# The first output projection's loads in another order, half of y kept in SBUF, and one norm's root moved to VectorE

## The chip, the cores and the metric

The kernel runs on one core of one Trainium2 chip. The metric is the device time of one execution in microseconds, and of several runs the median. Before the change the runs gave 3252.81, 3256.49 and 3258.94 us, so the median is 3256.49 us. Engines are named as the profile names them: PE is TensorE, DVE is VectorE, ACT is ScalarE, POOL is GpSimd, SP is SyncE, which here does nothing but issue transfers.

## The reference

`x` is (4, 1024, 512) in float32. One decoder block is computed: a Mamba layer with its MLP, a cross-attention on a context of 64 tokens, and a feed-forward layer with low-rank experts. A layer norm of the sum with the input closes each of the three. The change touches the first of them, which in short is:

```python
def _mamba(x, ...):
    xz = x @ in_proj_w.T
    u, z = jnp.split(xz, 2, axis=-1)               # 1024 features each
    u_act = silu(causal_conv(u))
    dt_r, Bm, Cm = jnp.split(u_act @ x_proj_w.T, [32, 48], axis=-1)
    dt = softplus(dt_r @ dt_proj_w.T + dt_proj_b)
    dA = exp(dt * A)                               # 16 states
    dBu = dt * Bm * u_act
    h_t = dA_t * h_{t-1} + dBu_t                   # lax.scan over the tokens
    y = sum_n(hs_n * Cm_n) + u_act * Dp
    return (y * silu(z)) @ out_proj_w.T
h = x + _mamba(_rmsnorm(x, norm1_w), ...)
xn = _rmsnorm(h, norm2_w)
h = h + (silu(xn @ w1.T) * (xn @ w2.T)) @ w3.T
```

`_rmsnorm` multiplies by the reciprocal root of the mean square plus 1e-5, and by a weight.

## The kernel before

**Chunks, groups, steps, quarters.** The 4096 tokens are worked on as 8 chunks `c` of 512. The 1024 features are two halves of 4 blocks of 128. One chunk and one half make a group `g = 2c + half`; one group and one of the 16 states make a step `k = 16g + n`, so there are 256 steps. A step has 4 quarters, one per block of features (and per block of 128 tokens). Quarters are counted through in `now[0]`, and this count is called a slot: slot = 4k + quarter.

**One quarter** is the function `quarter(k, q, other)`, and it does, in this order: PE turns a block of the step before (`turn`, tile `ps_h`), `other()` gives PE work of the MLP, DVE does one scan of 512 tokens (`scan`, tile `hs`, with the decay `da` as input), ACT makes a decay two blocks ahead (`exp`, tile `da`) and in some quarters puts in the state carried over (`carry_in`), the turned block is multiplied by C and added up in `acc`, and in the first two quarters POOL makes the input product of the next step (`times_b`, 128x1024 elements). Of the additions into `acc` most are made by DVE from PSUM; for some, ACT first makes the tile `hc` and POOL adds it, or PE adds it when turning back (tables `JS0`, `AS0`, `JS`, `AS`).

**The order is written out by hand.** `InOrder` ties each instruction of PE, ACT, DVE and POOL to the one issued before it on the same engine, so these four run in program order, and every instruction has the line number of that helper (308) in the profile. Transfers issued by SP are not tied; the scheduler places them, and SP's queue then runs in its order. Work for a later slot is registered with `at(d, phase, f)` and is run in the named phase of the quarter `d` slots later; the table `NP` has these delays for the MLP.

**The end of a group.** `end()` turns the sums back to features by tokens (`ps_y`), `add_u` on DVE adds the skip term, giving the tile `y`, and `times_z` on POOL multiplies by the gate. Then a transfer issued by ACT's queue one slot later writes the 128x512 tile to DRAM (`dr["y"]`, 256 KB); there are 64 of these in the run.

**The MLP stream.** `stream()` is a generator; each element is a group of matmuls with a cost, and `paced` hands out at most two per quarter while their cost stays under a budget (`PACE`). It makes for each chunk an `Mlp`, whose `__init__` loads `h` (1 MB, the chunk's `x`, line 854), whose `load_o` loads four tiles `wo` of 512 KB of the out projection's weight (line 869), and whose `load_y` reads back the chunk's `y` in four tiles `wy` of 512 KB (line 874). `wy` shares a ring of 5 buffers with the tiles `w12` of the MLP's weights (line 972). `out_proj` multiplies (`ps_o`, 4 blocks of tokens by 8 of features), then come the residual (`norm_h`, DVE, tile `hn`), the squares (`norm_sq`, ACT), the reciprocal root (`norm_r`, POOL, by `rsqrt_p`: a first guess from the bits and three Newton steps, on 128x4 elements), the scaling (`norm_x`, ACT), the addition (`norm_add`, POOL, tile `h`) and the turns (`turns`, tile `xn`). The first `Mlp` is made at slot 161:

```python
def stream():
    yield from until(GJ * 2 * NS + 33)
    mlp = Mlp(0)
```

The `Mlp` of a later chunk is made inside `run` of the one before, and its out projection starts at slot 128(c+1) + 21 or after. The last chunk's MLP runs after the scan, interleaved with the attention.

**Memory around the first MLP.** Up to step 39 the first chunk's turned-back parts `hc` are held in a pool of 44 buffers (`hz`), with a PSUM pool of its own (`zp`). It is closed after that step, and the pools of the MLP (`wp`, `xp`, `gp`, `sm`, `pp`) are opened in its place; a load into a tile there waits until the former user of the space has been read.

**Other lines that matter.** `load_b` (line 704) loads `b`, a row spread over 128 partitions; `load_uz` (line 787) loads skip and gate; `rsqrt_v` (line 189) is the root on DVE, with 12 small operations, and `rsqrt_p` (line 206) that on POOL, with 13.

Of the kernel before, what the change touches and what calls it, by code (L numbers as in the profile page):

```python
# [10 lines left out]
F32 = mybir.dt.float32  # L11
# [3 lines left out]
ALU = mybir.AluOpType  # L15
# [4 lines left out]
P = 128  # L20
B, L, D = 4, 1024, 512
N = B * L
KD = D // P
DI, KI = 1024, 8
NS = 16
DTR = 32
T = 512
NT = T // P
NC = N // T
# [108 lines left out]
for g, first in enumerate((4, 6)):  # L138
    for n in range(1, 16):
        for t in range(4):  # L140
            i = 4 * (n - 1) + t
# [8 lines left out]
EARLY_STEPS = 4  # L150
# [9 lines left out]
def f32(t):  # L160
    return t.bitcast(F32)
# [15 lines left out]
def rsqrt(nc, pool, out, v, tag):  # L177

    shape = list(out.shape)
    r = pool.tile(shape, F32, tag=tag + "r", name="rs_r")  # L180
    w = pool.tile(shape, F32, tag=tag + "w", name="rs_w")
    nc.scalar.activation(r, v, AF.Ln)
    nc.scalar.activation(r, r, AF.Exp, scale=-0.5)
    nc.vector.tensor_tensor(w, v, r, ALU.mult)
    nc.vector.tensor_tensor(w, w, r, ALU.mult)
    nc.vector.tensor_scalar(w, w, -0.5, 1.5, ALU.mult, ALU.add)
    nc.vector.tensor_tensor(out, r, w, ALU.mult)
# [18 lines left out]
def rsqrt_p(nc, pool, out, v, tag):  # L206

    shape = list(out.shape)
    r = pool.tile(shape, F32, tag=tag + "r", name="rs_r")
    w = pool.tile(shape, F32, tag=tag + "w", name="rs_w")  # L210
    nc.gpsimd.tensor_scalar(
        r.bitcast(I32), v.bitcast(I32), -0.5, float(0x5F3759DF), ALU.mult, ALU.add
    )
    for i in range(3):
        nc.gpsimd.tensor_tensor(w, r, r, ALU.mult)
        nc.gpsimd.tensor_tensor(w, w, v, ALU.mult)
        nc.gpsimd.tensor_scalar(w, w, -0.5, 1.5, ALU.mult, ALU.add)
        nc.gpsimd.tensor_tensor(out if i == 2 else r, r, w, ALU.mult)
# [43 lines left out]
def tokens(d, c, t=T):  # L262

    return d[c * t : (c + 1) * t].rearrange("(t p) d -> p t d", p=P)
# [17 lines left out]
def open_pool(tc, name, bufs, **kw):  # L282
    return tc.tile_pool(name=name, bufs=bufs, reuse_waits="tile", **kw)
# [374 lines left out]
def scan_mlp(tc, cn, a, dr, before, bx, then):  # L658
# [5 lines left out]
    nc = pin  # L664
    ident = cn["ident"]
    GJ = 4
    with ExitStack() as ctx, ExitStack() as sx:
# [8 lines left out]

        carry = cp.tile([P, KI, NS], F32, tag="carry", name="carry")
        pks, bs, cts, accs, hcs, uzs, firsts = {}, {}, {}, {}, {}, {}, {}
        zps, tw = [], []

        class Step:


            def __init__(self, k):
                self.k = k
                self.g, self.n = divmod(k, NS)
                self.c, self.half = divmod(self.g, 2)
                self.first = self.c % (L // T) == 0
                self.by_add, self.by_turn = (AS0[self.g], JS0[self.g]) if self.g < 2 else (AS, JS)
                self.da = {}  # L690
# [141 lines left out]

            def times_z(self, i, y):
                nc.gpsimd.tensor_tensor(y[1], y[1], uzs.pop((self.g, i))[:, 1], ALU.mult)
                jp, jj = divmod(GJ * self.half + i, 2)
                at(1, 3, nc.scalar.dma_start, dr["y"][self.c][jp][:, jj], y[1])
                if i < 2:
                    at(1, 3, self.load_uz, i + 2, nc.scalar)

        def at(d, phase, f, *args):  # L840

            due.setdefault((now[0] + d, phase), []).append(lambda: f(*args))
# [5 lines left out]
        class Mlp:  # L848


            def __init__(self, c):
                self.c = c
                self.h = xp.tile([P, NT, D], F32, tag="h", name="h", bufs=2)
                nc.sync.dma_start(self.h, tokens(a["x"], c))
                self.ws, self.ps, self.gs, self.w3s = {}, {}, {}, []

            def w3_tile(self, name, late):

                if late:
                    return tw[0].tile([P, 2, D], F32R, tag="w3", name=name)  # L860
                return wp.tile([P, 2, D], F32R, tag="w3", name=name, bufs=4)

            def load_o(self):
                self.wo, self.ys = [], []
                for jp in range(KI // 2):
                    if jp == KI // 4 and self.c == NC - 1:
                        self.load_y()
                    self.wo.append(f32(self.w3_tile("wo", self.c == NC - 1 and jp < 2)))
                    nc.sync.dma_start(self.wo[jp], a["w_out"][:, 2 * jp : 2 * jp + 2])

            def load_y(self):
                for jp in range(KI // 2):
                    self.ys.append(f32(wp.tile([P, 2, T], F32R, tag="w12", name="wy")))
                    nc.sync.dma_start(self.ys[jp], dr["y"][self.c][jp])

# [7 lines left out]
            def out_proj(self):  # L883

                self.ss = sm.tile([P, NT], F32, tag="ss", name="ss")
                self.r = sm.tile([P, NT], F32, tag="nr", name="nr")
                hn = [gp.tile([P, 2, T], F32R, tag="gs", name="hn", bufs=6) for i in range(2)]
                self.hn = [f32(hn[t // 2][:, t % 2]) for t in range(NT)]
                if not self.ys:
                    self.load_y()  # L890
                ys, ws = self.ys, self.wo
                for t in range(NT):
                    ps = pp.tile([P, D], F32, tag="mm", name="ps_o")
                    for j in range(KI):
                        jp, jj = divmod(j, 2)
                        nc.tensor.matmul(
                            ps, ys[jp][:, jj, t * P : (t + 1) * P], ws[jp][:, jj],
                            start=j == 0, stop=j == KI - 1,
                        )
                        if j == KI - 1:  # L900
                            at(*NP["h"], self.norm_h, t, ps)
                            at(*NP["s"], self.norm_sq, t)
                            at(*NP["a"], self.norm_add, t)
                            if t == NT - 1:
                                at(*NP["r"], self.norm_r)
                                for e in range(NT):
                                    at(*NP["x"][e], self.norm_x, e)
                                self.ready = now[0] + NP["t"]
                        yield MM32
# [8 lines left out]
                nc.scalar.activation(sq, self.hn[t], AF.Square, accum_out=self.ss[:, t : t + 1])  # L918

            def norm_r(self):  # L920
                nc.gpsimd.tensor_scalar(
                    self.ss, self.ss, 1.0 / D, 1e-5, ALU.mult, ALU.add
                )
                rsqrt_p(nc, sm, self.r, self.ss, "n")

            def norm_x(self, t):
                nc.scalar.activation(
# [160 lines left out]
        n = NC * 2 * NS  # L1088
# [65 lines left out]
        with ExitStack() as zx:  # L1154
            zps.append(zx.enter_context(open_pool(tc, "b_z", bufs=44, side="right")))
            zps.append(
                zx.enter_context(open_pool(tc, "b_zp", bufs=2, space=PSUM, side="right"))
            )
            for k in range(EARLY_STEPS, 2 * NS + 8):
                for q in range(GJ):  # L1160
                    quarter(k, q, lambda: None)
            turned[0] = 0
        wp = ctx.enter_context(open_pool(tc, "b_w", bufs=5, side="right"))
        xp = ctx.enter_context(open_pool(tc, "b_x", bufs=1, side="right"))
        gp = ctx.enter_context(open_pool(tc, "b_g", bufs=2, side="right"))
        sm = ctx.enter_context(open_pool(tc, "b_sm", bufs=2, side="right"))
        pp = ctx.enter_context(open_pool(tc, "b_p", bufs=3, space=PSUM, side="right"))

        def until(slot):
            while now[0] < slot:  # L1170
                yield 0

        def paced(gen):

            had = [0.0]

            def go():
                had[0] += PACE - TURN * turned[0]
                turned[0] = 0
                for _ in range(2):  # L1180
                    if had[0] <= 0:
                        break
                    cost = next(gen, 0)
                    if not cost:
                        had[0] = 0.0
                    else:
                        had[0] -= cost

            return go

        def first(mlp):
            mlp.load_o()
            yield from mlp.out_proj()
            yield from mlp.turns()

        def stream():
            yield from until(GJ * 2 * NS + 33)
            mlp = Mlp(0)
            yield from first(mlp)
            for c in range(NC - 1):  # L1200
                mlp = yield from mlp.run((lambda: Mlp(c + 1)) if c < NC - 2 else None)

        def last():
            mlp = Mlp(NC - 1)
            yield from first(mlp)
            yield from mlp.run()

        gen = stream()
        m = paced(gen)
        for k in range(2 * NS + 8, n + 2):  # L1210
            for q in range(GJ):
                quarter(k, q, m)

# [17 lines left out]
        sx.close()  # L1231
        tw.append(ctx.enter_context(open_pool(tc, "b_tw", bufs=2, side="right")))
        weave(alone(last()), then(pin, pp))


# [830 lines left out]
```

## Time and profile before

| | |
|---|---|
| median of three runs | 3256.49 us (3252.81 to 3258.94) |
| profiled execution, time | 3250.26 us |
| profiled execution, span | 3248.5 us |
| mean granted clock of PE | 0.959 |
| PE busy | 3001.8 us (92%) |
| DVE busy | 2698.2 us (83%) |
| POOL busy | 2369.2 us (73%) |
| ACT busy | 1973.4 us (61%) |
| transfers | 562.79 MB, mean 173 GB/s |

The profile is of one execution. Its page gives the busy time of each engine, the span in 40 slices of 81 us with the busy share of each engine in tenths, the chain of work that ended last, the costliest groups of instructions, and the transfers' issues. Register, branch and semaphore instructions and the issuing of transfers do not count as busy. Three phases can be told apart in the slices: the in-projection and convolution up to about 490 us, the scan with the MLP beside it up to about 2390 us, and then the last chunk's MLP with the attention and the expert layer. Beside the page, the trace answers for a stretch of time: the timeline of instructions, the waits and what ended them, and the busy time by window.

### The profile page before, as it was taken

What the parts mean: (1) busy time and instruction counts of PE and PEld (TensorE: products, weight loads), DVE (VectorE), ACT (ScalarE), POOL (GpSimd) and SP (SyncE); (2) the same over time, 40 slices, a digit from 0 to 9 for tenths busy, and PEclk for the clock granted to TensorE, in tenths of its full rate; (3) what the DMA queues carried; (4) which work ended last, traced back from release to release, by engine and by line L of the source; (5) the groups of instructions that cost most, each with busy time, mean ns of one, the idle gap of its engine ahead of it and who ended that gap; (6) DMA issues with size and microseconds to landing.
All of it is one profiled execution on the core that took longest, in us unless ns stands there. A gap on an engine that the chain in (4) does not pass through costs nothing.

```text
span 3248.5 us, 47327 instructions
## 1 busy us (share of the span) xinstructions
PE 3001.8 (92%) x15992; PEld 2393.6 (74%) x15992; DVE 2698.2 (83%) x3836; ACT 1973.4 (61%) x3876; POOL 2369.2 (73%) x2169
## 2 busy tenths in 40 slices
PE   7999996887999999999999999999999997999987
PEld 5777773664876786786776786786785887898876
DVE  6876767997999999999999999999962346888876
ACT  3666666776666567666667666667642336666643
POOL 1334328998998999999999999999952115666664
PEclk9999995778999999999999999999999999999998
DMA  4778744336675775675765765765766432111110
GB/s 165 261 264 288 256 167 163 111 104 215 198 224 179 221 223 179 220 226 178 221 223 175 225 217 177 225 213 172 219 190 228 142 104 95 46 46 47 48 41 33
DMA packets 478472, 562.79 MB, mean 173 GB/s; under 512 B 46006, under 2 KB 309814, under 8 KB 477974
## 3 DMA queue, kind: packets, MB, share of 16 engines
q1 hardware_dynamic: 464406, 526.21, 50.6%
q10 hardware_dynamic: 13824, 33.56, 3.2%
q8 instruction: 127, 2.08, 0.3%
q14 instruction: 115, 0.94, 0.1%
HBM read 430.18 MB, written 129.50 MB: 172 GB/s over the span
## 4 chain that ended last, share of the span: by engine, by line
PE 34%; DVE 23%; POOL 12%; issue 8%; DMA 4%; ACT 3%; SPq 0%; ACTq 0%; DVEq 0%; POOLq 0%
DVE hs L308 10%; PE ps_ab L308 10%; POOL hs L308 6%; DVE acc L308 5%; PE ps_m L308 5%; PE ps_h L308 5%; PE ps_o L308 3%; PE ps_s L308 3%; PE ps_b L308 2%; POOL acc L308 2%; PE ps_y L308 2%; DVE g L308 1%; ACT da L308 1%; DMA uz<-pk 1%; DMA w<-w 1%
## 5 line engine op out<-in xcount | busy, mean ns | idle before, releaser
L308 DVE TENSOR_TENSOR_SCAN hs<-da,hs 128x512 f32<-128x512 f32 x1024 | 1214.7, 1207 | 42.7 <-ACT da L308 21.3
L308 POOL TENSOR_TENSOR hs<-pk,b 128x1024 f32<-128x1024 f32 x512 | 1217.2, 2393 | 29.7 <-issue 10.5
L308 ACT ACTIVATE da<-pk,aneg 128x512 f32<-128x512 f32 x1024 | 704.9, 689 | 554.3 <-DVE hs L308 548.6
L308 PE MATMUL ps_ab<-xn,w 128*128 128x512 f32 x3072 | 827.6, 406 | 0.0
L308 PE MATMUL ps_h<-ident,hs 128*128 128x128 f32 x4096 | 684.8, 292 | 91.0 <-DVE hs L308 47.3
L308 PEld LDWEIGHTS ps_h<-ident,hs 128*128 128x128 f32 x4096 | 535.5, 149 | 313.9 <-DVE hs L308 80.5
L308 PEld LDWEIGHTS ps_ab<-xn,w 128*128 128x128 f32 x3072 | 545.0, 189 | 95.8 <-issue 1.1
L308 PE MATMUL ps_m<-w,gs 128*128 128x512 f32 x1536 | 419.3, 408 | 9.5 <-POOL gs L308 9.5
L308 DVE SCALAR_TENSOR_TENSOR acc<-ps_h,c,acc 128x512 f32<-128x512 f32 x542 | 394.2, 727 | 37.8 <-PE ps_h L308 35.6
L308 POOL TENSOR_TENSOR acc<-acc,hc 128x512 f32<-128x512 f32 x232 | 300.1, 1293 | 52.9 <-ACT hc L308 51.5
L308 PEld LDWEIGHTS ps_m<-w,gs 128*128 128x128 f32 x1536 | 274.4, 191 | 61.7 <-POOL gs L308 14.5
L308 PE MATMUL ps_o<-wo,wy 128*128 128x512 f32 x512 | 247.8, 602 | 8.4 <-DMA wy<-y 5.1
L308 ACT ACTIVATE hc<-ps_h,c 128x512 f32<-128x512 f32 x344 | 231.3, 673 | 12.6 <-PE ps_h L308 12.5
L308 POOL TENSOR_TENSOR gs<-g,gs 128x512 fp32r<-128x512 f32 x128 | 165.8, 1295 | 85.1 <-ACT gs L308 85.1
L308 PE MATMUL ps_in<-xn,wu 128*128 128x512 f32 x768 | 214.7, 428 | 0.1
L308 POOL TENSOR_TENSOR pt<-pw,pt 128x512 fp32r<-128x512 f32 x48 | 62.7, 1306 | 194.9 <-ACT pt L308 131.2
L308 PE MATMUL ps_in<-xn,wz 128*128 128x512 f32 x768 | 191.8, 397 | 1.0 <-POOL wz L308 0.6
L308 PEld LDWEIGHTS ps_in<-xn,wu 128*128 128x128 f32 x768 | 145.3, 190 | 56.9 <-issue 22.0
L308 PEld LDWEIGHTS ps_in<-xn,wz 128*128 128x128 f32 x768 | 142.4, 188 | 34.8 <-POOL wz L308 1.1
L308 DVE SCALAR_TENSOR_TENSOR cv<-ps_in,pvec,cv 128x509 f32<-128x509 f32 (+2 forms) x192 | 143.3, 746 | 7.0 <-ACT cv L308 2.3
L308 ACT ACTIVATE hs<-hs,first 128x1 f32<-128x1 f32 x512 | 120.4, 284 | 27.1 <-POOL hs L308 11.7
L308 PEld LDWEIGHTS ps_o<-wo,wy 128*128 128x128 f32 x512 | 87.9, 194 | 66.5 <-issue 65.9
(244 smaller groups left out, 4623.9 us busy)
## 6 DMA issues: line engine op xcount, KB each, us to landing
w<-w SPq DMA_DIRECT2D x384, 512.0 KB, 5.6
b<-b SPq DMA_DIRECT2D x256, 256.0 KB, 4.1
pk<-pk SPq DMA_DIRECT2D x64, 512.0 KB, 6.7
w<-pt SPq DMA_DIRECT2D x48, 512.0 KB, 3.2
pk<-z SPq DMA_DIRECT2D x64, 256.0 KB, 2.9
pk<-u SPq DMA_DIRECT2D x32, 512.0 KB, 3.9
pk<-r SPq DMA_DIRECT2D x32, 512.0 KB, 3.1
pk<-q SPq DMA_DIRECT2D x32, 512.0 KB, 3.7
```

The lines of the kernel that those rows point to most:

```text
L308: ins = f(*args, **kw)
```

## The change

The change has three parts.

1. The first `Mlp`'s loads. It is made at slot 156 instead of 161, and the order of its loads is now `wo`, `wy`, `h` instead of `h`, `wo`, `wy`. Its out projection starts at slot 160 instead of 161. For this, the pools `hz` and `zp` are closed one step earlier.
2. For chunks 0 to 6, the four tiles `y` of the second half of the features are not written to DRAM but kept in SBUF until the out projection reads them there. `load_y` reads back only the first half, in two tiles instead of four. The last chunk goes through DRAM as before.
3. The reciprocal root of the first chunk's MLP norm is made by DVE with `rsqrt_v`, 13 small operations with the one ahead of it, in place of 14 on POOL. The other chunks keep POOL.

```diff
-        zps, tw = [], []
+        zps, tw, kept = [], [], []
...
             def times_z(self, i, y):
                 nc.gpsimd.tensor_tensor(y[1], y[1], uzs.pop((self.g, i))[:, 1], ALU.mult)
-                jp, jj = divmod(GJ * self.half + i, 2)
-                at(1, 3, nc.scalar.dma_start, dr["y"][self.c][jp][:, jj], y[1])
+                if self.half and self.c < NC - 1:
+                    kept.append(y[1])
+                else:
+                    jp, jj = divmod(GJ * self.half + i, 2)
+                    at(1, 3, nc.scalar.dma_start, dr["y"][self.c][jp][:, jj], y[1])
...
             def __init__(self, c):
                 self.c = c
-                self.h = xp.tile([P, NT, D], F32, tag="h", name="h", bufs=2)
-                nc.sync.dma_start(self.h, tokens(a["x"], c))
+                if c:
+                    self.load_h()
...
+            def load_h(self):
+                self.h = xp.tile([P, NT, D], F32, tag="h", name="h", bufs=2)
+                nc.sync.dma_start(self.h, tokens(a["x"], self.c))
...
             def load_y(self):
-                for jp in range(KI // 2):
+
+                for jp in range(KI // 2 if self.c == NC - 1 else KI // 4):
...
-                ys, ws = self.ys, self.wo
+                ws = self.wo
+                ys = [y[:, jj] for y in self.ys for jj in range(2)]
+                while len(ys) < KI:
+                    ys.append(kept.pop(0))
...
-                            ps, ys[jp][:, jj, t * P : (t + 1) * P], ws[jp][:, jj],
+                            ps, ys[j][:, t * P : (t + 1) * P], ws[jp][:, jj],
...
             def norm_r(self):
-                nc.gpsimd.tensor_scalar(
-                    self.ss, self.ss, 1.0 / D, 1e-5, ALU.mult, ALU.add
-                )
-                rsqrt_p(nc, sm, self.r, self.ss, "n")
+                eng, rsqrt = (nc.gpsimd, rsqrt_p) if self.c else (nc.vector, rsqrt_v)
+                eng.tensor_scalar(self.ss, self.ss, 1.0 / D, 1e-5, ALU.mult, ALU.add)
+                rsqrt(nc, sm, self.r, self.ss, "n")
...
-            for k in range(EARLY_STEPS, 2 * NS + 8):
+            for k in range(EARLY_STEPS, 2 * NS + 7):
...
         def first(mlp):
-            mlp.load_o()
             yield from mlp.out_proj()
             yield from mlp.turns()
 
         def stream():
-            yield from until(GJ * 2 * NS + 33)
+            yield from until(GJ * 2 * NS + 28)
             mlp = Mlp(0)
+            mlp.load_o()
+            mlp.load_y()
+            mlp.load_h()
+            yield from until(GJ * 2 * NS + 32)
             yield from first(mlp)
...
         def last():
             mlp = Mlp(NC - 1)
+            mlp.load_o()
             yield from first(mlp)
             yield from mlp.run()
...
-        for k in range(2 * NS + 8, n + 2):
+        for k in range(2 * NS + 7, n + 2):
```

## The prediction

> **What bounds the kernel now.** I read the page from the slices down: where the span is full, and with what. POOL and DVE stand at 9 from slice 12 to slice 30, which is the scan of the state space (about 500 to 2390 us).
>
> ```profile
> span 3248.5 us, 47327 instructions
> ...
> DVE  6876767997999999999999999999962346888876
> ...
> POOL 1334328998998999999999999999952115666664
> ```
>
> Then busy time by stretch. The columns are start:end, length, busy time and instructions of PE, PEld, DVE, ACT and POOL, the granted clock, the DMA share and GB/s.
>
> ```profile
> 740.00:800.00 60.00, 49.33 (x186) 28.23 (x187) 44.23 (x49) 35.20 (x78) 49.11 (x41) 0.81 0.57 183
> 800.00:980.00 180.00, 176.86 (x990) 143.89 (x989) 174.89 (x202) 119.69 (x243) 171.79 (x95) 1.00 0.66 208
> 980.00:1225.00 245.00, 235.75 (x1271) 184.68 (x1270) 234.80 (x274) 155.17 (x297) 232.50 (x157) 0.99 0.67 207
> 1225.00:1469.00 244.00, 236.02 (x1267) 184.85 (x1266) 234.67 (x273) 164.11 (x339) 232.64 (x158) 0.99 0.67 207
> ```
>
> A settled chunk takes 244 to 245 us, with DVE busy for 234.8 and POOL for 232.5: both engines bound it together, PE close behind. One stretch is loose, 740 to 800: DVE 44.23 of 60. There the first output projection and the first MLP norm begin. Next, the waits of 735 to 800 (total, times, longest).
>
> ```profile
> DVE acc L308 <- PE ps_h L308: 9.5, 6, 7.7
> POOL acc L308 <- ACT hc L308: 6.5, 2, 3.8
> DVE hs L308 <- ACT da L308: 5.9, 3, 4.6
> PE ps_o L308 <- DMA wy<-y: 5.1, 2, 4.7
> ```
>
> The reader is to see two stalls: one where PE waits for `wy` (4.7 us) and DVE behind it (7.7), one where DVE waits for ScalarE's `da` (4.6), which turns out to lie behind the norm. In the settled chunks I find neither DVE nor POOL waiting for `wy` or for a write of `y`. So the change can act in these two places, and hardly elsewhere.
>
> **Part 1, the loads' order (first stall).** The timeline (start, duration, engine, operation, idle time before it):
>
> ```profile
> 726.67 0.43 SPq L854 DMA_DIRECT2D h<-in_x_dram  x1
> 727.15 1.59 SPq L869 DMA_DIRECT2D wo<-in_w_out_dram  x2
> 728.85 0.49 SPq L704 DMA_DIRECT2D b<-b  x1
> 729.39 1.22 SPq L869 DMA_DIRECT2D wo<-in_w_out_dram  x2
> 731.15 2.90 SPq L874 DMA_DIRECT2D wy<-y  x3
> ...
> 741.41 3.75 PE L308 MATMUL ps_o<-wo,wy 128*128 128x512 f32 x4 [4.69 <-DMA wy<-y]
> ...
> 748.86 0.75 DVE L308 SCALAR_TENSOR_TENSOR acc<-ps_h,c,acc 128x512 f32<-128x512 f32 x1 [7.72 <-PE ps_h L308]
> ```
>
> SP already sent all of it in one burst from 726.7, since the space of `wo`, `wy` and `h` is that of the in-projection's tiles, which PE's last `ps_y` passes release at 725.9 to 727.0. Those passes stay where they are. So asking five quarters sooner (a quarter here is about 1.75 us: 0.72 for `acc`, 1.21 for a scan less overlap) does not send them sooner; I give this no gain. What changes is the order: `h` (1 MB) goes from first to last, and the third and fourth `wy` are gone. By microsecond from 727 the profile moved 106, 238, 383, 322, 403, 414, 342, 352, 408, 399, 369, 418, 422, 420 and 408 KB, which is 5.2 MB by 741.4. Ahead of the end of the first `wy` now stand four `wo` and itself (2.6 MB), and the `uz`, `b` and `y` that share the 16 engines, put at 0.9 MB: 3.5 MB, which that curve reaches at 737.3; the second `wy` follows at about 738.6. PE gets to the first pass at about 735.6, so it waits until 737.2, not 741.41. From the first pass to the DVE product that had waited took 748.86 - 741.41 = 7.45 us at half clock. One quarter's four `ps_h` (0.60) come on top, the passes standing a quarter earlier in the order: 737.2 + 7.45 + 0.6 = 745.3. That is 3.5 us gained, and the last wait of 0.38 for the fourth `wy` also goes. The ends: 1 us if `uz` and `b` come ahead as much as now, 8.1 if the stall goes wholly (7.72 + 0.38). I take 3.9, by the curve. `h` at the end costs nothing: it is first read at the residual, some 50 quarters later. Two `b` tiles, sent at 728.85 and 736.54, now stand behind `wy`; POOL's products that follow start at 740.62 and 748.89, and no wait of POOL for a transfer is in the list. Bounds 0 to +1, taken 0.
>
> The granted clock was 1.00 until 733, 0.50 from 734 to 747 and 0.97 then: it came back 5.6 us after the passes began at 741.4. I use this row, which moves with the passes. The Trainium skill (TensorE: Matmul & The Clock Gate, Part 1) says the array returns to full rate after about 3.4 us of sustained work; going by it the last 2.2 us at half rate would count for half, and the stall would gain 1.1 us more. The trace's 5.6 us does not agree, and nothing in the sum uses the page.
>
> **Part 2, y in SBUF.** Seven chunks lose 28 issues of `y` on ScalarE's queue (0.33 us each there) and 14 of `wy` on SP (512 KB each), 14 MB in all. Beside: ScalarE is busy for 155 to 164 of 245 us, the DMA engines for 0.67 of the time, and SP is off the path. All DVE waits for ScalarE's `da` come to 21.3 us in the whole run, 6.2 of them in 735 to 800 with the neighbouring ones; 28 x 0.33 = 9.2 us of ScalarE time could take some of the rest, at most 3 us. On the other side, the kept tile of the last block is written by POOL at 735.61 to 736.90, and PE reads it after four passes at the earliest (737.2 + 3.75); if POOL were late, one product of 1.29 us. Bounds -3 to +1.3; taken 0, as no wait in a settled chunk names it. The buffer of `y` is used again 64 quarters later, which leaves no wait.
>
> **Part 3, the norm's root (second stall).** Before, POOL made it in 14 small operations 0.28 us apart, 787.44 to 791.29, and DVE ran on beside it:
>
> ```profile
> 787.44 0.19 POOL L308 TENSOR_SCALAR ss<-ss 128x4 f32<-128x4 f32 x1 [2.79 <-ACT sq L308]
> ...
> 791.33 1.33 ACT L308 ACTIVATE hn<-hn,nr 128x512 f32<-128x512 f32 x2 [1.23 <-POOL nr L308]
> ...
> 796.00 1.22 DVE L308 TENSOR_TENSOR_SCAN hs<-da,hs 128x512 f32<-128x512 f32 x1 [4.62 <-ACT da L308]
> ```
>
> Now 13 small DVE operations stand in DVE's order ahead of the scans that ran from 784.20, and every scan behind them waits for ScalarE's `sq` and for the chain. A free small DVE operation is 0.16 to 0.17 us, 0.20 apart. But elsewhere in this trace such an operation does not run while POOL is in a two-input product:
>
> ```profile
> 3188.14 2.67 POOL L308 TENSOR_TENSOR et<-ef,et 128x512 fp32r<-128x512 f32 x2
> ...
> 3188.54 0.91 DVE L308 TENSOR_SCALAR ln_v<-mv 128x2 f32<-128x2 f32 x1
> ...
> 3189.49 0.17 DVE L308 TENSOR_SCALAR rs_w<-ln_v 128x2 int32<-128x2 int32 x1
> ...
> 3189.69 1.14 DVE L308 TENSOR_SCALAR rs_r<-rs_w 128x2 int32<-128x2 int32 x1
> ```
>
> Each ends when POOL's product ends; one slips in between two products. A 128x1024 product at 144.49 (2.41) held a DVE product from 145.25 for 2.20 us likewise, where others take 0.69. The scans are not held: 1024 of them have a mean of 1207 ns. POOL, rid of the root, goes on with `h` (1.27) and 128x1024 products of 2.35 each: on the clock of before, one ends at 784.65, `h` at 785.9, then 788.25 and 790.6. `sq` ended at 787.35 and now stands a quarter sooner in the order, some 2.3 us here: about 785.0. So: the first operation ends at 786.0, the second slips in, the third ends at 788.3, the fourth slips in, the fifth ends at 790.6, where POOL must wait for a `hc` that needs DVE; eight more at 0.20 give 792.2. The scan of 784.20 then starts at 792.2, 8.0 us late. Idle time that stood there before (0.76 + 4.62 + 0.48 + 0.37 = 6.2) takes part of that back; not all, as ScalarE's `da`, `hc` (0.68 each), `hs` (0.48) and four `hn` (0.67) still come in their order. Followed forward, the scan of 796.00 comes at 801.3 and that of 804.85 at 809.1: 4.3 us lost. The lower end: nothing held, the chain ends at 785.0 + 13 x 0.20 = 787.6 and ScalarE's order sets the rest, -0.6 to +0.4. The upper: one product more in the way, +2.35, so +6.6. I take 4.3, from the rows of the held operations.
>
> The Trainium skill (Perfetto Trace Analysis) warns that moving work between GPSIMD and DVE might not help, as they share a read port. Taken as "no gain" it would put this part at 0, and the sum at -3.9; the rows make it a loss.
>
> **The sum.** -3.9 + 0 + 4.3 = +0.4 us. The profiled execution has a span of 3248.5 and a time of 3250.26; the median of the three runs, 3256.49, is 6.2 (0.19%) above it. 3250.7 as a profiled execution is 3256.9 as a median.
>
> **Rivals.** *Faster: the first stall goes, and the port does not bite.* Place: 735.6. If the first `wy` is there when PE comes, the gain is 8.1. The curve has moved 2.8 MB by 735.6, and four `wo` with one `wy` are 2.6 MB: it needs the queue to let them pass almost alone. Against: `uz` and a `y` leave at 726.30, ahead of them. With the root at its free price (+0.4 to -0.6) and up to 3 from part 2: -7.7 to -11.7, so 3244.8 to 3248.8. For: POOL also waits here (6.5 us for `hc`), and while it waits nothing is held.
>
> *Slower: POOL's products hold the root all the way.* One mechanism: if each product lets only two small operations through, 13 of them need six products, 6 x 2.35 = 14.1 us, not the 7.2 counted; that is 6.9 more, 3263.8. It decides from three further products on (7.05). For: two per product is what the rows show. Against: POOL's `acc` must wait for `hc`, `hc` for `ps_h`, that for a scan, and the scan stands behind the root on DVE; so POOL runs dry after the second or third product.
>
> *The loads do not do what the change says.* If `wo` and `wy` still come behind `h` and `b` through the release of space, part 1 is 0 and the sum +4.3: 3260.8, still within 0.2%.
>
> **How the numbers follow.** 0.2% of the time, 6.5 us, is about what a measurement of this kernel can tell from no change. The likeliest case, both stalls nearly balanced, with the third rival in it: 0.46, 3252 to 3262. The faster rival, or parts of it such as the first stall gone and half of the root's cost: 0.32. The slower: 0.22. The range leaves out a tenth on each side: low, 3245, is the faster rival with all of part 2; high, 3265, is the slower one with the late `b`.
>
> **What would show it.** Right: `wo` before `h` on SP from about 726.7; the first `ps_o` pass near 737; DVE's 7.7 us wait down to about 4; near 785 small DVE operations of 0.9 to 2.3 us that end with POOL products, and scans late by 8; settled chunks of 244 to 245 us as before. Wrong if the small operations all take 0.2 us, if the loads leave before 725, or if a settled chunk is shorter.

## The result and the profile after

The changed kernel takes 3259.75 us (median of 22 runs, 3255.57 to 3267.58), the kernel before 3252.52 us (22 runs beside it, 3249.16 to 3259.30). The ratio is 1.0021, with a 95% interval of 1.0015 to 1.0026: 7.2 us slower by the medians. The prediction's time, 3256.9, and its sum of +0.4 us belong to a time before of 3256.49, the median of the three runs then known. Ratios here and below are the record's; they differ a little from the quotient of the two medians beside them.

The timeline around the first stall, after the change (start, duration, engine, operation, idle time before it and what ended it):

```profile
728.01 2.06 SPq L876 DMA_DIRECT2D wo<-in_w_out_dram  x4
...
730.11 1.16 SPq L882 DMA_DIRECT2D wy<-y  x2
...
731.32 0.44 SPq L868 DMA_DIRECT2D h<-in_x_dram  x1
...
739.18 3.78 PE L308 MATMUL ps_o<-wo,wy 128*128 128x512 f32 x4 [1.90 <-DMA wy<-y]
...
743.86 0.75 DVE L308 SCALAR_TENSOR_TENSOR acc<-ps_h,c,acc 128x512 f32<-128x512 f32 x1 [4.21 <-PE ps_h L308]
...
747.97 0.75 DVE L308 SCALAR_TENSOR_TENSOR acc<-ps_h,c,acc 128x512 f32<-128x512 f32 x1 [1.11 <-PE ps_h L308]
```

The order on SP is that of the change, and it starts at 728.0, not five quarters ahead of the old 727.15. This execution runs 1.4 us later than the profiled one of before already ahead of the stall, so the first pass comes at 737.8 on the clock of before, 3.6 us sooner. DVE's long wait is 4.2 us, where it was 7.7; a second one of 1.1 us follows.

The second stall, after the change:

```profile
783.97 6.08 DVE L308 TENSOR_SCALAR ss<-ss 128x4 f32<-128x4 f32 x1 [1.20 <-ACT sq L308]
784.18 1.25 POOL L308 TENSOR_TENSOR h<-h,hn 128x512 f32<-128x512 f32 x1
...
785.40 4.63 POOL L308 TENSOR_TENSOR hs<-pk,b 128x1024 f32<-128x1024 f32 x2
...
790.09 0.17 DVE L308 TENSOR_SCALAR rs_w<-ss 128x4 int32<-128x4 int32 x1
...
792.15 3.44 DVE L308 TENSOR_TENSOR_SCAN hs<-da,hs 128x512 f32<-128x512 f32 x3
...
798.74 1.28 POOL L308 TENSOR_TENSOR acc<-acc,hc 128x512 f32<-128x512 f32 x1 [8.71 <-ACT hc L308]
```

A multiplication of four numbers per partition took 6.08 us. It starts while the product ahead of them still runs (781.87 to 784.22), and ends when POOL's three products, back to back, end at 790.0. Twelve small operations of 0.17 us follow, and the scans go on at 792.15. Then POOL, which had run ahead, idles for 8.7 us, waiting for a product that hangs on those scans.

Two settled chunks, by window (busy time and instructions of PE, PEld, DVE, ACT, POOL; granted clock; DMA share; GB/s):

```profile
980.00:1225.00 245.00, 234.14 (x1266) 182.78 (x1266) 234.14 (x273) 153.52 (x294) 232.34 (x157) 1.00 0.63 198
1225.00:1469.00 244.00, 232.85 (x1258) 182.57 (x1257) 232.08 (x271) 162.59 (x339) 230.10 (x155) 0.99 0.64 198
```

The DMA share fell from 0.67 to 0.63 or 0.64. But the second window holds 271 DVE instructions where it held 273, and 232.1 us of their work in place of 234.7: this chunk has become slower, though no single wait in it is long.

**A table by stages.** Because the code ahead of and behind the scan is the same, I compare the starts of the scans in the traces. They are counted from 0 as they run, one per slot; scan 150 lies ahead of the first stall, 180 between the stalls, 300 well behind the second, 1023 is the last. Each column is how much longer a stage took than in the first profile of before, in us.

| kernel | to 150 | 150 to 180 (first stall) | 180 to 300 (second stall) | 300 to 1023 (later chunks) | after the scan | span |
|---|---|---|---|---|---|---|
| before, again | +1.3 | +0.15 | +0.01 | -0.11 | +0.8 | +2.1 |
| changed | +1.4 | -2.45 | +5.80 | +5.22 | -1.8 | +8.2 |
| changed, again | +0.8 | -1.98 | +5.77 | +4.94 | -1.0 | +8.6 |

The loss has three terms, not two: a gain of 2.5 us, a loss of 5.8, and a loss of 5.2 in the chunks behind. What lies outside the scan moves by a few us from one execution to the next with the same code; the three terms don't.

The first row and the last are two runs made for this:

> The changed kernel a second time, for a second profile. If the stages' differences to the kernel before are properties of the programs, they come out the same within 0.5 us: first stall -2.5, second stall +5.8, later chunks +5.2, while the in-projection ahead of the scan, whose code is the same, may differ by up to 4 us. Rival (these differences are scatter of one execution): they move by 2 us or more.

> The kernel before a second time, for a second profile. If the stages' lengths are properties of the program, each of the three differences to the first profile of this kernel is within 0.5 us of zero. Rival (scatter of one execution): 2 us or more in some stage of the scan.

Measured: as expected from properties of the programs, each stage within 0.5 us. So for one kernel a stage repeats to half a microsecond. Between kernels less can be read: further down the root alone has +0.83 at the first stall, where it changes nothing, and the kernels whose out projection starts at slot 161 lie between -1.39 and +1.31 in the later chunks. Differences of 2 us and more stand out from that.

### The profile page after: what moved, and what is told of

It reads as the page before. It is cut to its first block, busy times and chain, and to the rows that moved or that the text cites. A ratio compares the mean times of both kernels' runs of the same rounds, so it can differ in the third digit from the quotient of the medians.

```text
span 3256.7 us, 47248 instructions
## 1 busy us (share of the span) xinstructions
PE 3001.8 (92%) x15992; PEld 2393.5 (73%) x15992; DVE 2707.4 (83%) x3849; ACT 1971.2 (61%) x3876; POOL 2367.2 (73%) x2155
## 4 chain that ended last, share of the span: by engine, by line
PE 37%; DVE 23%; POOL 9%; issue 8%; ACT 4%; DMA 3%; SPq 0%; ACTq 0%; DVEq 0%; POOLq 0%
DVE hs L308 11%; PE ps_ab L308 10%; PE ps_o L308 5%; PE ps_h L308 5%; PE ps_m L308 5%; DVE acc L308 5%; POOL hs L308 4%; PE ps_s L308 3%; PE ps_b L308 2%; PE ps_y L308 1%; POOL acc L308 1%; DMA uz<-pk 1%; DVE g L308 1%; ACT da L308 1%; PE ps_num L308 1%
## 5 line engine op out<-in xcount | busy, mean ns | idle before, releaser
L308 PE MATMUL ps_o<-wo,wy 128*128 128x512 f32 x288 | 137.3, 608 | 4.7 <-DMA wo<-in_w_out_dram 2.8
L308 POOL TENSOR_TENSOR q<-r,u 128x1024 f32<-128x1024 f32 x32 | 76.6, 2394 | 78.0 <-issue 31.9
```

The source lines that it names most:

```text
L308: ins = f(*args, **kw)
```

## The experiments

First the parts apart.

| kernel | time, us (before beside it) | ratio, 95% interval | first stall | second stall | later chunks |
|---|---|---|---|---|---|
| loads alone | 3258.07 (3252.26) | 1.0011 (1.0002 to 1.0020) | +2.80 | -2.32 | +2.35 |
| y kept alone | 3250.30 (3252.26) | 0.9990 (0.9981 to 0.9999) | -0.76 | +0.23 | -1.28 |
| root alone | 3255.14 (3252.26) | 1.0008 (0.9999 to 1.0017) | +0.83 | +2.36 | +0.08 |
| loads and y kept | 3249.09 (3252.26) | 0.9995 (0.9986 to 1.0003) | -1.99 | -0.43 | +2.64 |
| changed, root in PSUM | 3256.35 (3251.92) | 1.0017 (1.0008 to 1.0026) | -2.44 | +2.24 | +5.18 |
| order and y kept, slot 161 | 3244.96 (3251.92) | 0.9979 (0.9970 to 0.9988) | -3.67 | +0.05 | -0.31 |
| loads and y kept, h first | 3248.48 (3251.92) | 0.9988 (0.9979 to 0.9997) | -1.25 | -2.21 | +2.48 |
| order and y kept, slot 161, root in PSUM | 3246.25 (3251.92) | 0.9983 (0.9974 to 0.9992) | -3.33 | +0.15 | -1.39 |
| early loads, y kept, out projection at 161 | 3245.47 (3252.35) | 0.9978 (0.9967 to 0.9988) | -3.96 | +0.45 | -0.61 |
| order and y kept, slot 161, root as changed | 3249.21 (3252.35) | 0.9988 (0.9980 to 0.9997) | -3.72 | +3.15 | +1.31 |

**Loads alone.** The change without the kept tiles and without the root. As the last tiles of y are written only shortly before, the second half of `wy` is asked for when the fifth pass needs it (the second `load_y` below; the first reads only the first half):

```diff
             mlp = Mlp(0)
+            mlp.load_o()
+            mlp.load_y()
+            mlp.load_h()
+            yield from until(GJ * 2 * NS + 32)
...
+                        if jp == len(ys):
+                            self.load_y()
```

> Only the first part: the first MLP's loads sent from slot 156 in the order wo, the first two wy, h; the out projection from slot 160; all of y still goes through DRAM and its second half is read back when the fifth pass asks for it; root on POOL. By my account the first stall alone changes: scans from slot 164 on stand 2.5 us earlier against those of slot 160 than before, as in the changed kernel, unless the late wy takes up to 2 us of it; the time falls by 0.5 to 2.5 us (ratio 0.9992 to 0.9998). Rival (the shift of the stream by a slot costs in the later chunks): the scans lose some 5 us between slots 384 and 640 and the time rises by 2 to 3 us.

Measured: 1.0011, slower, against my account. The first pass is early, and then PE waits for the last `wy`, which SP sends at 745.14, after ACT's queue has written the y that it reads (sent at 738.65):

```profile
739.46 3.75 PE L308 MATMUL ps_o<-wo,wy 128*128 128x512 f32 x4 [1.79 <-DMA wy<-y]
...
752.65 2.05 PE L308 MATMUL ps_o<-wo,wy 128*128 128x512 f32 x2 [3.56 <-DMA wy<-y]
...
755.59 0.75 DVE L308 SCALAR_TENSOR_TENSOR acc<-ps_h,c,acc 128x512 f32<-128x512 f32 x1 [5.38 <-PE ps_h L308]
```

So the first part needs the second: the last tile of y comes too late for an early out projection if it goes through DRAM, and the stall is only moved. The rival was right about the later chunks (+2.35).

**y kept alone.** The old order and slot, with the second half of y in SBUF:

```diff
+                if self.half and self.c < NC - 1:
+                    kept.append(y[1])
...
-                for jp in range(KI // 2):
+                for jp in range(KI // 2 if self.c == NC - 1 else KI // 4):
```

> Only the second part: the second half's y kept in SBUF, two wy read back in place of four; loads at slot 161 with h first, root on POOL. By my account nothing but the last wait of 0.4 us in the first stall goes; the settled chunks stay at 244 to 245 us; ratio 0.9990 to 1.0005. Rival (the kept tiles cost in the later chunks, where the changed kernel lost 5 us between slots 384 and 640): time up by 4 to 6 us, ratio 1.0012 to 1.0018.

Measured: 0.9990, a small gain at the edge of what can be told (the interval ends at 0.9999), and the later chunks lose nothing. The rival falls: the 5.2 us there don't come from the kept tiles.

**Root alone.** Only `norm_r` of the first chunk changed:

```diff
+                eng, rsqrt = (nc.gpsimd, rsqrt_p) if self.c else (nc.vector, rsqrt_v)
...
```

> Only the third part: the first norm's root on VectorE. By my account this is the loss: one small VectorE operation is held for 5 to 6 us by POOL's products h and hs, x2, the scans after the root are 8 us late, and after slot 200 some 5.5 us of it stay; time up by 4 to 7 us, ratio 1.0012 to 1.0022. Rival (the loss lies in the other parts and the root is taken up by idle time): ratio within 0.0006 of 1.

Measured: 1.0008, which by its interval fits the rival (up to 1.0006) as well; the second stall decides, at +2.36 us. The sign is as expected, the size is half: here `sq` came later against POOL, and `ss` was held for 3.09 us, not 6.

**Loads and y kept.** The change with the root back on POOL.

```diff
-                eng, rsqrt = (nc.gpsimd, rsqrt_p) if self.c else (nc.vector, rsqrt_v)
-                eng.tensor_scalar(self.ss, self.ss, 1.0 / D, 1e-5, ALU.mult, ALU.add)
-                rsqrt(nc, sm, self.r, self.ss, "n")
+                nc.gpsimd.tensor_scalar(
+                    self.ss, self.ss, 1.0 / D, 1e-5, ALU.mult, ALU.add
+                )
+                rsqrt_p(nc, sm, self.r, self.ss, "n")
```

> The first two parts, root on POOL as before. By my account the gain of the first stall without the loss of the second: time down by 2 to 4 us, ratio 0.9988 to 0.9995, and no VectorE operation of 6 us near 784. Rival (5 us lost in the later chunks belong to these parts): time up by 2 to 3 us, ratio 1.0006 to 1.0010.

Measured: 0.9995. Both accounts are half right: 2 us gained at the first stall, and 2.6 us lost in the later chunks. Against the changed kernel the second stall is 6.2 us shorter, so that is the price of the root in this order.

**Why is the small operation held?** The changed kernel, with the root's tiles laid so that no operation has two inputs in SBUF, or its input and its output there:

```diff
+                    ps = pp.tile([P, D], F32, tag="mm", name="ps_r")
+                    v, w = (ps[:, NT * i : NT * i + NT] for i in range(2))
+                    r = sm.tile([P, NT], F32, tag="nr_r", name="rs_r")
...
+                        tt(w, v, r, ALU.mult)
+                        tt(w, w, r, ALU.mult)
+                        nc.vector.scalar_tensor_tensor(
+                            self.r if i == 2 else r, w, 1.5, r, ALU.add, ALU.mult
+                        )
```

> The changed kernel, but the 13 root operations on VectorE work on tiles in PSUM and SBUF, each with at most one input and not both its input and its output in SBUF. Theory (POOL's products keep VectorE off the shared SBUF port): the first operation near 784 takes about 0.2 us and not 6.1, the root ends near 787.5 instead of 792.2, the scans of slots 183 to 186 come 4 to 5 us sooner, and the time falls against the changed kernel by 4 to 9 us, to a ratio of 0.9995 to 1.0010 to the kernel before. Rival (the hold comes from something else, such as a wait that the profile counts into the operation): the first operation again takes 5 to 6 us and the ratio stays at 1.0015 to 1.0026.

```profile
784.68 0.17 DVE L308 TENSOR_SCALAR ps_r<-ss 128x4 f32<-128x4 f32 x1 [1.20 <-ACT sq L308]
784.87 1.25 POOL L308 TENSOR_TENSOR h<-h,hn 128x512 f32<-128x512 f32 x1
...
785.48 0.37 DVE L308 TENSOR_TENSOR ps_r<-ps_r,rs_r 128x4 f32<-128x4 f32 x2
...
786.09 4.64 POOL L308 TENSOR_TENSOR hs<-pk,b 128x1024 f32<-128x1024 f32 x2
...
787.18 3.44 DVE L308 TENSOR_TENSOR_SCAN hs<-da,hs 128x512 f32<-128x512 f32 x3
```

The hold is gone: 0.17 us beside the same POOL products, and the scans go on at 787.2, 5 us sooner (5.7 counted from scan 180). That the hold hangs on where the operands lie is shown by taking it away; that a shared port does it is not shown by a row. The Trainium skill (SBUF — State Buffer, section "Who interferes with whom") states that a VectorE instruction with at most one SBUF input outside its two-port modes does not contend with GpSimd; these rows agree. But the time fell by less than expected, and by the times alone the two kernels can't be told apart (1.0017, 1.0008 to 1.0026, against 1.0021). The second stall is 3.6 us shorter than in the changed kernel, and still +2.24. The rest is not the hold: VectorE waits 1.2 us for `sq` and spends 2.5 us on the root, and in this order its idle time does not take that up; why it doesn't was not tested.

**Order alone, at the old slot.** Kept y and the order `wo`, `wy`, `h`, all at slot 161, root on POOL:

```diff
             yield from until(GJ * 2 * NS + 33)
             mlp = Mlp(0)
+            mlp.load_o()
+            mlp.load_y()
+            mlp.load_h()
             yield from first(mlp)
```

> Half of y kept and the loads in the order wo, wy, h, but at slot 161 as before, the out projection from slot 161, and the root on POOL. Theory (the order gains at the first stall, and the stream standing a slot earlier costs 2.7 us in chunks 2 and 3): the first stall gains 2 to 4 us against the kernel before, nothing drifts between slots 384 and 640, time down by 3 to 6 us, ratio 0.9982 to 0.9992, faster than with the loads at slot 156. Rival (the loads must be asked for early): no gain at the first stall, ratio 0.9990 to 1.0000, as with kept y alone.

Measured: 0.9979, faster than both kernels; 3.7 us gained at the first stall and no drift. The stall's rows:

```profile
741.60 3.78 PE L308 MATMUL ps_o<-wo,wy 128*128 128x512 f32 x4 [2.22 <-DMA wy<-y]
...
748.46 0.75 DVE L308 SCALAR_TENSOR_TENSOR acc<-ps_h,c,acc 128x512 f32<-128x512 f32 x1 [4.69 <-PE ps_h L308]
```

This execution runs 2.65 us late ahead of the stall, so its first pass comes at 738.95 on the clock of before (741.41 there). With `h` first and y kept it is 744.00 - 2.58 = 741.42. The order, with the kept tiles, gains 2.5 us of waiting for data.

**Early, but h first.**

```diff
+            mlp.load_h()
             mlp.load_o()
             mlp.load_y()
-            mlp.load_h()
```

> The first two parts, root on POOL, the loads at slot 156 and the out projection at slot 160, but h ahead of wo and wy. Theory (the space is released at about 726, so asking sooner does nothing, and the order alone gains): the first pass of the out projection comes 2 to 3 us later than with h last, VectorE waits 6 to 8 us in the first stall, ratio 0.9998 to 1.0010. Rival (being asked for sooner is what gains): the first pass as early as with h last, ratio 0.9988 to 0.9998.

Measured: the first pass at 741.89 - 2.10 = 739.79, 1.6 us later than with `h` last (742.63 - 4.46 = 738.17), and the first stall gains 0.7 us less; VectorE's wait is 6.0. The direction is as expected, the size of the first is below the 2 to 3 us. The time is not as expected: 0.9988, no slower than with `h` last, and in the rival's range. Its second stall came out 1.8 us shorter, which the account didn't foresee; the granted clock was 0.50 there for 10.2 us, as in the loads alone with their -2.32, and for 17.1 us with `h` last. No run changes that clock alone. The early place does bring something for the first pass, which comes 1.6 us sooner than with `h` first at slot 161 (741.42): `wo` and `wy` then go ahead of a `b`.

**Early, but the out projection at slot 161.** Against "loads and y kept" one line differs:

```diff
-            yield from until(GJ * 2 * NS + 32)
+            yield from until(GJ * 2 * NS + 33)
             yield from first(mlp)
```

> The first two parts with the root on POOL, the loads at slot 156 in the changed order, but the out projection from slot 161 as before. Theory (what costs in chunks 2 and 3 is that the stream of the MLP stands a slot earlier from the first out projection on): the first stall gains 2 to 4 us, nothing drifts between slots 300 and 640, ratio 0.9975 to 0.9990, like the kernel with the order alone. Rival (the early loads and the pool closed a step sooner bring the drift): scans lose 2.5 us between slots 300 and 640, ratio 0.9988 to 1.0000.

Measured: 0.9978, later chunks -0.61. This one line separates the drift from the loads: with the stream at slot 160 the later chunks lose 2.35 to 2.64 us in three kernels with the root on POOL; at slot 161 they lose none. Asking early does send something sooner: the first pass comes at 742.62 - 4.73 = 737.89, 1.1 us ahead of the 738.95 above, since a `b` that SP sent ahead of `wy` at 731.37 there goes behind it here (735.42). But the first stall gains hardly more (3.96 against 3.67).

**The root at the old slot, free and held.** The kernel with the order alone, with the root in PSUM as above, and with the root as in the change:

> As the kernel with the order alone (loads at slot 161, h last, y kept), and the first norm's root on VectorE with tiles in PSUM. Theory (without the hold the root on VectorE costs about what POOL's costs beside it): within 2 us of the kernel with the order alone, ratio 0.9978 to 0.9995, no VectorE operation over 0.5 us in the root. Rival (VectorE is the loser of the move in any case, since its scans wait behind sq): 3 to 5 us slower than the order alone, ratio 0.9993 to 1.0007.

> As the kernel with the order alone (slot 161, h last, y kept), with the first norm's root on VectorE in SBUF, as in the change. Against the same with the root in PSUM only the hold by POOL differs. Theory: the first operation is held for 2 to 6 us; the second stall costs 2 to 4 us more than with the root in PSUM; ratio 0.9986 to 1.0000. Rival (the hold costs only where the out projection stands at slot 160): no difference from the root in PSUM, ratio 0.9976 to 0.9988.

The second, held:

```profile
787.92 3.23 DVE L308 TENSOR_SCALAR ss<-ss 128x4 f32<-128x4 f32 x1 [1.98 <-ACT sq L308]
...
793.24 4.56 DVE L308 TENSOR_TENSOR_SCAN hs<-da,hs 128x512 f32<-128x512 f32 x4
```

Measured: 0.9983 and 0.9988. The times don't tell the two apart, but the second stall does: +0.15 free, +3.15 held. At this slot the root on VectorE costs nothing measurable if POOL can't hold it, and nothing is gained by it either.

## Why the prediction was right or wrong

The measured time, 3259.75 us, lies in the range, 2.9 us above the number given, and in the 3252 to 3262 of the likeliest case. Part of that is luck. The kernel before took 3252.52 us in the runs beside it, 4.0 us less than the median from which the prediction started. As a difference, +7.2 us was measured where +0.4 was forecast, and "both stalls nearly balanced" does not describe it: 0.21%, slower. Term by term:

- **What the change can reach.** "So the change can act in these two places, and hardly elsewhere" is the step that failed. 5.2 us were lost in chunks behind, whose order I had only checked for the waits that the change removes. I had seen that the stream stands one slot earlier, and priced the move only at the first stall (0.6 us). The line with `until` shows that it costs about 2.5 us later on; by what mechanism stays open. A second 2.6 us appear when the root is on VectorE as well (+5.2 in the changed kernel and +5.2 with the root in PSUM), although in the scan the order on the four engines is the same with the root on either engine, but for the root itself. It is no scatter of one execution, as the second profile shows. The last section has the place where 1.5 us of it arise.
- **Part 1, the order.** Right in mechanism: SP sends the loads from 728.01, which is 726.6 on the clock of before (726.67 there), and the order decides. The gain was put at 3.9 and measured 2.5. The first pass was put at 737.2 and came at 737.8. The larger part is the term for the passes standing a quarter earlier: from the first pass to the DVE product that had waited (now the one at 747.97) it took 8.79 us, not 7.45 + 0.6. At slot 161 the same loads gained 3.7 to 4.0.
- **Part 2.** Taken as 0, bounds -3 to +1.3; alone it measured 2.0 us by the medians, 1.8 by the scans, of which 1.28 lie in the later chunks and are within what kernels scatter there. I missed its other role: without it the order gains nothing (1.0011).
- **Part 3, the root.** Right in mechanism; the time of day agreed by luck. The scans were put at 792.2 and came at 792.15, but at scan 180 this execution stood 1.03 us ahead of the one before, so on the clock of before they came at 793.2, 9.0 us late and not 8.0. "The second slips in" between two products was wrong: nothing slipped in, a single operation was held over all three. So twelve operations and not eight were left when the products ended (2.1 us, put at 1.6), and the products ended half a microsecond later than put. The stall was put at 4.3 and measured 5.8, within the bound of 6.6. The lower bound, "nothing held ... -0.6 to +0.4", holds at slot 161 (+0.15) and not in the changed order (+2.24).
- **The slower rival** named the right place, but POOL ran dry after the third product, as the counter-argument said (8.7 us idle). The rest of the loss came from the later chunks.
- **The clock.** The granted clock was 0.50 from 735 and back at 1.00 in the window from 745, 5.7 us after the passes began at 739.2, as the row of before had it (5.6). In each profile here the granted clock changes only on a grid of 3.41 us. In both kernels the passes began 1.1 to 1.2 us into an interval of that grid, and the clock came back at the end of the next whole one: 2.25 + 3.41 = 5.66. The Trainium skill (TensorE: Matmul & The Clock Gate, Part 1) means its 3.4 us as one busy window, and says that the window is free-running. So rule and rows agree, and "does not agree" in the prediction read the page too narrowly; no term of the sum rested on it.

## What to carry to other kernels

A small VectorE operation from SBUF to SBUF isn't small beside a GpSimd engine that runs two-input products back to back: in the norm it waited for the end of the run (6.08, 3.09 and 3.23 us), and everything behind it in VectorE's order waits too, though the prediction's rows show one operation that slipped in between two products. Put one operand or the result in PSUM (0.17 us), or leave the work where it is. In an order written out by hand, moving a stream by one slot moves it for all that follows; price the chunks behind, not only the place where it was moved. When loads are released by space, not by their issue, what can be gained is their order, and the bytes taken out ahead of the first one needed.

## What the runs showed that was not expected

A chunk's length depends on how the MLP stream stands against the scan. By the starts of the scans, slots 384 to 512 take 243.2 to 244.3 us in the kernels with the out projection from slot 161, 245.1 to 245.2 with the stream a slot earlier and 245.8 to 246.0 with the root on VectorE besides. The arithmetic instructions are the same, and no new wait stands out: in the changed kernel no single wait of DVE in these slots is longer than 1.9 us (1.7 before).

In the chunk after that, one place can be named. Of the 2.6 us that the changed kernel loses against "loads and y kept", 1.5 arise between scans 566 and 570, where PE waits for POOL's product `gs`. First "loads and y kept", then the changed kernel:

```profile
1523.43 0.51 PE L308 MATMUL ps_m<-w,gs 128*128 128x512 f32 x1 [0.98 <-POOL gs L308]
1523.77 0.60 PE L308 MATMUL ps_h<-ident,hs 128*128 128x128 f32 x4
```

```profile
1526.78 0.80 PE L308 MATMUL ps_m<-w,gs 128*128 128x512 f32 x1 [2.29 <-POOL gs L308]
1527.38 1.05 PE L308 MATMUL ps_h<-ident,hs 128*128 128x128 f32 x4
```

In the changed kernel the granted clock was 0.50 from 1526.5 to 1529.9, in the other 1.00 at these passes; its stretch at 0.50 had come earlier in the chunk, from 1516.4 to 1519.9. The second profile of the changed kernel and that with the root in PSUM show the same as the first (PE waits 2.29 and 2.27 us, four `ps_h` take 1.06 and 1.05). So PE at half clock goes together with more than half of the second loss. No run changes the clock alone, and why the stretch falls where it does, and where the other 1.1 us come from, stays open.

Executions with the same code ahead of the scan start it up to 4.5 us apart, while the scan's stages of one kernel repeat to 0.5 us. So a single profile told effects of 2 us and more apart, stage by stage, that the times, with intervals of a thousandth, could not.
